# Expert tiles cut into three places of two turns, short VectorE operands moved to PSUM, and sorting spread over odd turns

## Chip, core and metric

The kernel runs on one core of a Trainium2 chip. The metric is the device time of one execution in microseconds; of several runs the median is given. Five engines work from queues of their own, each in order: TensorE (PE; its weight loads are the rows PEld), VectorE (DVE), ScalarE (ACT), GpSimd (POOL) and SyncE (SP), which here only issues DMAs.

## What is computed

Eight images of 256 channels and 32 x 32 places go through two layers. All is float32.

```python
# layer 0: deformable attention, 4 heads, 64 sampled keys per image
x = x + conv_attn(groupnorm(x))
#   logits get a bias per (query, key): a perceptron of width 64 on the
#   signed log distance, 2 -> 64 -> 64 -> 1, for 1024 x 64 pairs and 4 groups
# layer 1: on 1024 tokens of 256 per image
t = t + attn(layernorm(t))          # sigmoid(q t^T) t, no softmax
t = t + moe(layernorm(t))           # 8 experts 256 -> 256 -> 256, top 2 of a router
#   moe(u) = u + sum_e weight_e * (gelu(u w1[e] + b1[e]) w2[e] + b2[e])
```

The bias perceptron is most of the arithmetic.

## The kernel before

**Turns.** The main loop runs over 8 batches (images) of 64 turns. A turn does two steps of the bias perceptron. For each, a first layer `h1` of 128 x 1024 values is made two turns ahead: one by GpSimd (L471) with a ReLU on ScalarE (L476), one by VectorE (L469). TensorE runs the second layer, eight small products into the two PSUM buffers `h2p` (L484). They are emptied by ScalarE (L490) for the first kind and VectorE (L492) for the second. In even turns the third layer follows (`sim`, L511). A turn with nothing else on TensorE (an odd one, "bare" below) has 2 us of matmuls; an even one has 3.9. The perceptron's inputs `ta` and `nb` come by DMA every eight turns and are scaled in `scale` (L440 to L442) when the turn's number leaves 3 by 8: `ta` on ScalarE, `nb` on VectorE.

**Work beside it.** Everything else is cut into steps by generators (each `yield` ends a step), and the loop says which step stands at which turn. Every engine then works in exactly the order in which the program was written (`in_order`, L76); only the order of the scattering DMAs among themselves is free. In batch b these run:
- `prep` of batch b+1 (L236): group norm, queries, a 36-tap convolution on VectorE (L285, L287), offsets and sampling. `Side.step` (L1011) runs it and the softmaxes of batch b, from turn 5; while `sorting` is set, it runs no step of `prep`.
- `attention` of batch b-1 (L600): `to_query` (layer norm, transposes, projections), `slots` (the products `ap` and `vp`), `finish` (second layer norm, router logits), then `route` (L798), the sorting: it picks two experts per token, counts, and gives each token a slot. It is some 45 short VectorE operations on 8 to 168 columns, in six steps. Then 16 scattering DMAs on GpSimd (L781), one a turn, send the tokens to their slots.
- `experts` of batch b-2 (L893): 12 rounds of two tiles of 128 slots (the last batch: 15 of one tile of 256). Round n, as one step, runs `yp` for n-2 (L928; second product, emptied by VectorE's `yt`, L933), fetches and weight loads (L907, L914), `hp` for n-1 (L946; first product, emptied by the gelu `ht`, L954), and `tp` for n (L964; transposes, emptied by ScalarE's `xg`, L966).
- `combine` of the batch before that (L971): gathers on GpSimd (L999), VectorE's weighted sums (L991), transposes `op` (L982), stores. One step a turn.

`mix` (L1074) says when a step of `experts` is due: in batches 2 to 6 at turns 24, 26, 27, 29, 31 and 33 and at odd turns from 41 to 57, and the last at turn 9 of the next batch. It leaves out 35, 37 and 39, where the sorting stands. In batch 7 it runs a step at turns over 9 that are odd or divisible by 3. After turn 63 the tail does the last attention, sorting and experts.

All small matmul outputs (`psum`, L129) share a pool of two PSUM banks, taken in turn: each waits until what was written two takes before has been read. One more bank, `still` (L138), holds copies of `nb` in its first half; its second half (`shared`) is the convolution's and the sorting's workspace.

Of the kernel before, what the change touches and what calls it, by code (L numbers as in the profile page):

```python
# [9 lines left out]
F32 = mybir.dt.float32  # L10
I32 = mybir.dt.int32
AF = mybir.ActivationFunctionType
ALU = mybir.AluOpType
# [90 lines left out]
def tile_conv_attn_hybrid(ctx: ExitStack, tc: tile.TileContext, x, par, qw, w1, w2_, cst, out):  # L104
# [34 lines left out]
    held_nb = still[:, 0:256].rearrange("p (s g y) -> p s g y", g=2, y=16)  # L139
    shared = still[:, 256:512]  # L140
    attending = sorting = convolving = False

    def xin(b):
# [43 lines left out]


    ncb2 = cpool.tile([P, 1], F32, name="ncb2")
    nc.vector.tensor_scalar(ncb2, par_("cb2"), -1.0, None, ALU.mult)  # L190
# [45 lines left out]
    def prep(b, xb, st):  # L236
        qp = frames[b % 2]
        stats = small.tile([P, 2, 2, 6], F32, name="stats")
        mv = small.tile([P, 2, 2], F32, name="mv")
        for k in range(2):  # L240
            for h in range(2):
                nc.vector.bn_stats(stats[:, k, h, :], xb[:, k, halves(h)])
            nc.vector.bn_aggr(mv[:, k, :], stats[:, k, :, :].rearrange("p h s -> p (h s)"))
            yield
        gm = psum("gm")
        nc.tensor.matmul(gm[:, 0:2], lhsT=cst_("gavg"), rhs=mv[:, :, 0], start=True, stop=True)
        gmean = small.tile([P, 2], F32, name="gmean")
        nc.vector.tensor_copy(gmean, gm[:, 0:2])
        dm = small.tile([P, 2], F32, name="dm")
        nc.vector.tensor_sub(dm, mv[:, :, 0], gmean)  # L250
        nc.vector.tensor_mul(dm, dm, dm)
        nc.vector.tensor_add(dm, dm, mv[:, :, 1])
        yield
        gv = psum("gv")
        nc.tensor.matmul(gv[:, 0:2], lhsT=cst_("gavg"), rhs=dm, start=True, stop=True)
        grs = small.tile([P, 2], F32, name="grs")
# [169 lines left out]
    def terms(b, k, h, part):  # L426
        number = 4 * k + 2 * h + part
        fd = sts[b]["fd"].rearrange("k (s r) f -> k r s f", r=2)
        ta = abpool.tile([P, 16, 2, 32], F32, name="ta")
        nb = abpool.tile([P, 16, 2, 16], F32, name="nb")  # L430
        nc_ = abpool.tile([P, 2, 8, 16], F32, name="nc")
        taf = ta.rearrange("p s g x -> p s (g x)")
        nbf = nb.rearrange("p s g y -> p s (g y)")
        ss = slice(part * 16, (part + 1) * 16)
        for r in range(2):
            rs = slice(64 * r, 64 * r + 64)
            nc.sync.dma_start(out=taf[rs], in_=fd[k, r, ss, 0:64].partition_broadcast(64))
            nc.sync.dma_start(out=nbf[rs], in_=fd[k, r, ss, 64 + 32 * h : 96 + 32 * h].partition_broadcast(64))

        def scale():  # L440
            nc.scalar.activation(taf, taf, AF.Identity, bias=par_("cb1"), scale=par_("w1x"))
            nc.vector.tensor_scalar(nbf, nbf, par_("w1y"), -1.0, ALU.mult, ALU.mult)  # L442

        def second():
            cps = [psum("cp") for _ in range(2)]
            for r, g in ((0, 0), (1, 1), (0, 1), (1, 0)):
                rs, gs = slice(64 * r, 64 * r + 64), slice(64 * g, 64 * g + 64)
                nc.tensor.matmul(
                    cps[r][gs, 0:128], lhsT=par_("w2")[rs, gs], rhs=nb[rs, 1::2, g, :],
                    start=True, stop=True, tile_position=(64 * r, 64 * g),  # L450
                )
            for r in range(2):
                nc.scalar.activation(  # L453
                    nc_[:, r].rearrange("p s y -> p (s y)"), cps[r][:, 0:128], AF.Identity, bias=ncb2,
                )

        def hold(half):
            nc.scalar.copy(held_nb[:, 4 * half : 4 * half + 4], nb[:, 8 * half + 1 : 8 * half + 8 : 2])  # L458

        return (ta, nb, nc_, b, number), scale, second, hold  # L460
# [139 lines left out]
    def attention(b, st, o, rt):  # L600
# [8 lines left out]
        def to_query(h):  # L609
# [18 lines left out]
            yield  # L628
            mv = small.tile([P, 4, 2], F32, name="lmv")
            for u in range(4):  # L630
# [36 lines left out]
        def finish(q):  # L667
            mv = small.tile([P, 2, 2], F32, name="lmv2")
            for u in range(2):
# [83 lines left out]
        def rest():  # L753
# [20 lines left out]
            attending = sorting = True  # L774
            yield from route(lqs, rt, LARGE if b == NB - 1 else SMALL)
            attending = sorting = False

            xs, group = xss[b % 2], f"slots{b}"
            for n in range(16):
                m, c = divmod(n, 2)  # L780
                sent = nc.gpsimd.indirect_dma_start(  # L781
                    out=xs[:, :], out_offset=bass.IndirectOffsetOnAxis(ap=rt["slot"][:, c, m : m + 1], axis=0),
                    in_=ut[:, m, :], in_offset=None,
                )
                if n:
                    tc.declare_no_dep(sent.ins, group=group, reason="other slots")
                tc.add_to_no_dep_group(group, sent.ins)
                sents.add(sent.ins.name)
                yield
            rt.update(xs=xs, xu=xu)  # L790
# [7 lines left out]
    def route(lqs, rt, slots_):  # L798
# [8 lines left out]

        def part(n, size=64):
            a = shared[:, 64 * n : 64 * n + size]
            return a.rearrange("p (m e) -> p m e", e=E) if size == 64 else a  # L810

# [9 lines left out]
        def pick(name):  # L821
            m = one.tile([P, 8], F32, name="m" + name)
            nc.vector.tensor_reduce(m, lg, AX.X, ALU.max)
            eq, first = part(1), part(2, 8)
            nc.vector.tensor_tensor(eq, lg, wide(m), ALU.is_equal)
# [31 lines left out]
        )  # L857
        many = one.tile([P, E], F32, name="many")
        nc.vector.tensor_reduce(many, need, AX.X, ALU.add)
# [3 lines left out]
        nc.vector.tensor_reduce(ends[:, 1:9], part(1), AX.X, ALU.add)  # L863
        at = part(3)
        nc.vector.scalar_tensor_tensor(
# [3 lines left out]
        for c in range(2):  # L869
            nc.vector.tensor_scalar(ws[c], m1, 0.5 - c, 0.5, ALU.mult, ALU.add)  # L870
        place = one.tile([P, 2, 8], F32, name="place")
        for c, oh in enumerate((oh1, oh2)):
            nc.vector.tensor_tensor(part(1), at, oh, ALU.mult)
            nc.vector.tensor_reduce(place[:, c], part(1), AX.X, ALU.add)
        slot = held("slot", (P, 2, 8), I32)
        nc.vector.tensor_copy(slot, place)
        yield
# [4 lines left out]
        )  # L882
        whose = one.tile([P, TILES], F32, name="whose")
        nc.vector.tensor_reduce(whose, which, AX.X, ALU.add)
        expert = held("expert", (P, TILES), I32)
        nc.vector.tensor_copy(expert, whose)
        yield
        rt.update(slot=slot, expert=expert, w=ws)

# [3 lines left out]
    def experts(b, rt):  # L893
# [23 lines left out]
        fetch(0)  # L917
        yield
        fetch(1)
        first[0] = weights(0, w1pool, 2 * C + 2, w1, "w1")  # L920
        yield
        for n in range(rounds + 2):
            if n >= 2:
# [9 lines left out]
                nc.vector.tensor_tensor(yt, yp, f2[:, 0:several, 2 * C :].to_broadcast([P, 2, C]), ALU.add)  # L933
                nc.sync.dma_start(out=yv[at(n - 2), :].rearrange("(s p) c -> p s c", p=P), in_=yt)  # L934
            if n + 2 < rounds:
                fetch(n + 2)
# [20 lines left out]
            if n + 1 < rounds:  # L957
                first[n + 1] = weights(n + 1, w1pool, 2 * C + 2, w1, "w1")
            if n < rounds:
                xl = rows.pop(n)  # L960
# [5 lines left out]
                nc.scalar.copy(xg, tp)  # L966
            if n < rounds + 1:
                yield
        sums.append((b, combine(b, rt, yv)))
# [35 lines left out]
    class Side:  # L1005
# [5 lines left out]
        def step(self, both=True):  # L1011
            busy = False
            if self.waiting and not (sorting and self.busy):
                busy = self.busy
                self.busy = next(self.waiting[0], None)
                if self.busy is None:
                    self.waiting.pop(0)
                    self.busy = True
            if self.left and both and not busy and not sorting:
                self.left = next(self.prep, self) is not self  # L1020
# [52 lines left out]

    def mix(b, i):  # L1074
        of = mixtures[0][0] if mixtures else NB
        if of == b - 2 and b < NB - 1:
            due = i in (24, 26) or i > 26 and i % 2 and i not in (35, 37, 39, 59, 61, 63)
        elif of == b - 3:
            due = i == 9
        else:  # L1080
            due = b == NB - 1 and (i >= TURNS - 2 if of == b - 1 else of < b and i > 9 and (i % 2 or i % 3 == 0))
        if due:
            step(mixtures)

    def step(what):
        if what and next(what[0][1], what) is what:
            what.pop(0)

    for n in range(NB * TURNS):
        b, i = divmod(n, TURNS)  # L1090
        if i == 0:
            steps = iter(())
# [16 lines left out]
        if n % 8 == 6 and coming_ < total:  # L1109
            table = coming  # L1110
        new = []
        if n + 2 < NB * TURNS:
# [6 lines left out]
        if coming_ < total:  # L1119
# [5 lines left out]
            elif n % 8 == 6:  # L1125
                hold(1)
        if i > 4:
            side.step(i > (8 if b else 4))
# [7 lines left out]
        advance(mains)  # L1136
        mix(b, i)
        step(sums)
# [5 lines left out]
    while mains:  # L1144
        advance(mains)
        if sorted_ or not attending and n % 2:
            step(mixtures)
        sorted_ = sorted_ or sorting
        n += 1
    while mixtures:  # L1150
        step(mixtures)
        step(sums)
# [110 lines left out]
```

## Time and profile before

| what | value |
|---|---|
| median of 3 runs | 3119.95 us (3118.14 to 3121.78) |
| the profiled execution, its own time | 3118.0 us |
| its span, first to last instruction | 3116.2 us |
| head, up to the first second-layer matmul | 72.4 us |
| batches 0 to 7 (7: up to 6 us after turn 63 began) | 256.1, 320.6, 358.8, 366.1, 365.6, 369.3, 365.0, 372.8 us |
| tail | 269.6 us |
| granted TensorE clock, mean | 0.976 |
| GpSimd's L471, 128 x 1024, 512 times | 1916 ns each |
| VectorE's L469 and L492, 512 times each | 1212 and 1222 ns each |
| ScalarE's L476 and L490, 512 times each | 1051 and 1115 ns each |
| VectorE's L442 (`nb`), 64 times | 69.7 us, mean 1088, shortest 469, longest 2953 ns |

A page of the profile names a group of instructions by its line, engine, operation and tiles, as `out<-in`. It gives the time that the group was busy, the mean of one in ns, the idle time of its engine just ahead of it, and who ended that. A line of waits reads: who waited, for whom, us in total, how often, the longest. A line of the timeline reads: start and length in us, engine, line, operation, tiles, shape, how many in a row, and in brackets the idle time ahead of it with its releaser. A window's columns are busy times by engine with the number of instructions, then the clock, the share of DMA time and GB/s. Busy matmuls are modelled ends; idle time of an engine that is not the bound costs nothing.

### The profile page before, as it was taken

What the parts mean: (1) busy time and instruction counts of PE and PEld (TensorE: products, weight loads), DVE (VectorE), ACT (ScalarE), POOL (GpSimd) and SP (SyncE); (2) the same over time, 40 slices, a digit from 0 to 9 for tenths busy, and PEclk for the clock granted to TensorE, in tenths of its full rate; (3) what the DMA queues carried; (4) which work ended last, traced back from release to release, by engine and by line L of the source; (5) the groups of instructions that cost most, each with busy time, mean ns of one, the idle gap of its engine ahead of it and who ended that gap; (6) DMA issues with size and microseconds to landing.
All of it is one profiled execution on the core that took longest, in us unless ns stands there. A gap on an engine that the chain in (4) does not pass through costs nothing. (4 is left out here: it accounts for less than half of the span.)

```text
span 3116.2 us, 51813 instructions
## 1 busy us (share of the span) xinstructions
PE 2827.7 (91%) x19592; PEld 1397.0 (45%) x19592; DVE 1987.2 (64%) x3015; ACT 1851.2 (59%) x2662; POOL 1381.8 (44%) x945
## 2 busy tenths in 40 slices
PE   3889998899999999999999999999989999988965
PEld 2223443344445453544545444454545546425754
DVE  4887668765774777566775667757775564593212
ACT  3676655765676656765566665666567566555322
POOL 2554434643454544535454353545445343371132
PEclk7999999999999999999999999999999999999988
DMA  3321111211463234622346125542246245442376
GB/s 98 92 46 35 21 28 31 73 21 35 112 180 97 45 86 110 199 52 56 99 137 188 33 53 139 146 130 41 67 120 191 58 107 168 138 99 85 111 247 220
DMA packets 428297, 311.21 MB, mean 100 GB/s; under 512 B 284432, under 2 KB 368656, under 8 KB 428048
## 3 DMA queue, kind: packets, MB, share of 16 engines
q1 hardware_dynamic: 415472, 273.14, 32.9%
q0 software_dynamic: 12288, 33.57, 3.7%
q8 instruction: 154, 2.52, 0.4%
q10 hardware_dynamic: 288, 1.20, 0.1%
q14 instruction: 95, 0.78, 0.1%
HBM read 239.93 MB, written 67.90 MB: 99 GB/s over the span
## 5 line engine op out<-in xcount | busy, mean ns | idle before, releaser
L471 POOL TENSOR_TENSOR h<-ta,nb 128x1024 f32<-128x1024 f32 x512 | 980.5, 1916 | 1138.2 <-PE h2p L484 1040.4
L484 PE MATMUL h2p<-h,pr__101 64*64 64x512 f32 x8192 | 1023.1, 610 | 89.6 <-DVE h L492 60.7
L492 DVE TENSOR_TENSOR h<-h2p,nc 128x1024 f32<-128x1024 f32 x512 | 625.5, 1222 | 439.6 <-PE h2p L484 434.1
L490 ACT ACTIVATE h<-h2p,pr__101 128x1024 f32<-128x1024 f32 x512 | 571.0, 1115 | 474.9 <-PE h2p L484 473.7
L469 DVE TENSOR_TENSOR h<-ta,still 128x1024 f32<-128x1024 f32 x512 | 620.4, 1212 | 47.3 <-ACT still L458 44.4
L476 ACT ACTIVATE h<-h 128x1024 f32<-128x1024 f32 x512 | 538.0, 1051 | 34.5 <-POOL h L471 34.1
L484 PEld LDWEIGHTS h2p<-h,pr__101 64*64 64x64 f32 x8192 | 254.8, 133 | 619.5 <-issue 290.6
L511 PE MATMUL sim<-h,pr__101 128*32 128x512 f32 x4096 | 498.6, 605 | 0.0
L511 PEld LDWEIGHTS sim<-h,pr__101 128*32 128x32 f32 x4096 | 107.7, 110 | 367.7 <-issue 367.7
L717 PE MATMUL ap<-qt,tn 128*128 128x256 f32 x1024 | 251.1, 389 | 2.6 <-DVE x L739 1.0
L954 ACT ACTIVATE ht<-hp,w 128x128 f32<-128x128 f32 (+1 forms) x366 | 108.6, 377 | 242.0 <-PE hp L946 208.6
L727 PE MATMUL vp<-tt,sg 128*128 128x256 f32 x1024 | 233.0, 381 | 3.5 <-ACT nc L453 3.3
L928 PE MATMUL yp<-w,ht 128*128 128x256 f32 x792 | 198.4, 394 | 29.2 <-ACT ht L954 6.8
L717 PEld LDWEIGHTS ap<-qt,tn 128*128 128x128 f32 x1024 | 184.6, 190 | 86.9 <-issue 41.7
L999 POOL DMA_INDIRECT gs<-ys,slot x128 | 129.0, 1008 | 208.3 <-issue 64.9
L727 PEld LDWEIGHTS vp<-tt,sg 128*128 128x128 f32 x1024 | 193.2, 190 | 36.9 <-issue 5.7
L946 PE MATMUL hp<-xg,w 128*128 128x128 f32 (+1 forms) x1464 | 198.0, 288 | 12.0 <-PE yp L928 6.0
L739 DVE TENSOR_TENSOR x<-x,vp 128x512 f32<-128x512 f32 x64 | 44.0, 688 | 246.4 <-PE vp L727 246.4
L946 PEld LDWEIGHTS hp<-xg,w 128*128 128x128 f32 x1464 | 187.3, 194 | 29.3 <-PE yp L928 10.3
L928 PEld LDWEIGHTS yp<-w,ht 128*128 128x128 f32 x792 | 145.7, 193 | 87.5 <-issue 35.2
L933 DVE TENSOR_TENSOR yt<-yp,w 128x512 f32<-128x512 f32 x99 | 68.0, 687 | 167.6 <-PE yp L928 141.6
L735 ACT ACTIVATE sg<-ap 128x512 f32<-128x512 f32 x128 | 76.4, 598 | 148.0 <-PE ap L717 136.0
(270 smaller groups left out, 2611.1 us busy)
## 6 DMA issues: line engine op xcount, KB each, us to landing
w<-in_w SPq DMA_DIRECT2D x183, 384.0 KB
w<-in_w SPq DMA_DIRECT2D x183, 257.0 KB
ta<-fd SPq DMA_DIRECT2D x128, 256.0 KB
xl<-xs SPq DMA_DIRECT2D x99, 256.0 KB
ys<-yt SPq DMA_DIRECT2D x99, 256.0 KB
nb<-fd SPq DMA_DIRECT2D x128, 128.0 KB
xb<-in_x SPq DMA_DIRECT2D x8, 1024.0 KB
x<-in_x SPq DMA_DIRECT2D x8, 1024.0 KB
```

The source lines that it names most:

```text
L469: nc.vector.tensor_tensor(h1, a, b, ALU.max)
L471: nc.gpsimd.tensor_tensor(h1, a, b, ALU.subtract)
L476: nc.scalar.activation(h1, h1, AF.Relu)
L484: nc.tensor.matmul(h2p[gs, r, :], lhsT=par_("w2")[rs, gs], rhs=h1[rs, g].rearrange("p y x -> p (y x)"), start=True, stop=True, tile_positi ...
L490: nc.scalar.activation(h2, h2p, AF.Relu, bias=par_("cb2"))
L492: nc.vector.tensor_tensor(h2.rearrange("p r (y x) -> p r y x", x=W), h2p.rearrange("p r (y x) -> p r y x", x=W), nc_.unsqueeze(3).to_broad ...
L511: nc.tensor.matmul(sim[32 * q : 32 * q + 32, :], lhsT=par_("z3")[:, 15 - m : 47 - m], rhs=h2s[2 * u + q // 2][:, q % 2, :], start=False, s ...
L717: nc.tensor.matmul(ap[:, u, :], lhsT=tn[:, k, m0 : m0 + P], rhs=qt[:, k, quarter(q)], start=(k == 0), stop=(k == 1),)
L727: nc.tensor.matmul(vp[:, i, :], lhsT=sgs[s][:, u, i * P : (i + 1) * P], rhs=tt[:, 2 * todo[n - 2 + s][1] + u, :], start=(s == u == i == 0) ...
L928: nc.tensor.matmul(yp[:, s, :], lhsT=ht[:, f, s * P : (s + 1) * P], rhs=f2[:, s * several // 2, f * C : (f + 1) * C], start=(f == 0), stop ...
L946: nc.tensor.matmul(hp[:, f, us], lhsT=f1[:, u, k * C + f * P : k * C + (f + 1) * P], rhs=xg[:, k, us], start=(k == 0), stop=(k == 1),)
L999: nc.gpsimd.indirect_dma_start(out=got[m][:, c, :], out_offset=None, in_=yv[:, :], in_offset=bass.IndirectOffsetOnAxis(ap=slot[:, c, m : m ...
```

## The change

1. *Places of a tile.* `experts` yields three times a round: after `yp`, after `hp`, after `tp`. `mix` is called twice a turn, ahead of the turn's first and second layer (part 0) and at its end (part 1). In batches 2 to 6 the first fetches stand at turn 26. At each odd turn from 31 to 55, `yp` stands ahead of the second layer, fetches, weights and `hp` at the turn's end, and `tp` at the end of the next even turn. The last `yp` stands ahead of turn 9's second layer in the next batch. In batch 7 and in the tail, `whole()` runs three steps in one.
2. *Sorting.* `route` has five steps, at odd turns only (35 to 43), except in the tail. Its last part (which expert a tile has) runs between the second and third send. The sends start at turn 44. `Side.step` isn't run in the odd turns of the sorting, and `prep` is no longer held in the even ones.
3. *Short operands.* Twelve-column pieces `tiny` of `still`, and pieces `few` and `whose`, take the place of SBUF tiles: group means, layer norm statistics, the sorting's small vectors. The scaling of `nb` goes to ScalarE.

```diff
+    tiny = [still[:, 464 + 12 * n : 476 + 12 * n] for n in range(4)]
...
+        gmean, dm = tiny[3][:, 0:2], tiny[3][:, 2:4]
...
-        nc.vector.tensor_sub(dm, mv[:, :, 0], gmean)
-        nc.vector.tensor_mul(dm, dm, dm)
-        nc.vector.tensor_add(dm, dm, mv[:, :, 1])
+        nc.vector.tensor_sub(dm, mv[:, :, 0], gm[:, 0:2])
+        away = small.tile([P, 2], F32, name="away")
+        nc.vector.tensor_sub(away, mv[:, :, 0], gm[:, 0:2])
+        nc.vector.tensor_mul(dm, dm, away)
+        nc.vector.tensor_add(mv[:, :, 1], dm, mv[:, :, 1])
...
-            nc.vector.tensor_scalar(nbf, nbf, par_("w1y"), -1.0, ALU.mult, ALU.mult)
+            nc.scalar.activation(nbf, nbf, AF.Identity, scale=nw1y)
...
-            mv = small.tile([P, 4, 2], F32, name="lmv")
+            mv = tiny[2][:, 0:8].rearrange("p (u s) -> p u s", s=2)
...
-            yield from route(lqs, rt, LARGE if b == NB - 1 else SMALL)
+            steps = route(lqs, rt, LARGE if b == NB - 1 else SMALL)
+            for _ in range(5):
+                while b < NB - 1 and turn % 2 == 0:
+                    yield
+                next(steps)
+                yield
...
+                if n == 1:
+                    run(steps)
...
-            eq, first = part(1), part(2, 8)
+            eq, first = part(1), few(0)
...
-        many = one.tile([P, E], F32, name="many")
+        many = few(8)
...
-        place = one.tile([P, 2, 8], F32, name="place")
+        place = tiny[2][:, 0:8], tiny[3][:, 0:8]
...
-        whose = one.tile([P, TILES], F32, name="whose")
+        whose = shared[:, 168 : 168 + TILES]
...
         fetch(0)
-        yield
         fetch(1)
...
+            if n == rounds + 1:
+                break
+            yield
             if n + 2 < rounds:
                 fetch(n + 2)
...
                 first[n + 1] = weights(n + 1, w1pool, 2 * C + 2, w1, "w1")
+            yield
             if n < rounds:
...
-            if self.left and both and not busy and not sorting:
+            if self.left and both and not busy:
...
+    def mix(b, i, part):
         of = mixtures[0][0] if mixtures else NB
+        if b == NB - 1 and of >= b - 2:
+            if part and (i >= TURNS - 2 if of == b - 1 else i > 9 and (i % 2 or i % 3 == 0)):
+                whole()
+        elif of == b - 2:
+            if not part:
+                due = i in ODD
+            else:
+                due = i == 26 or i in ODD or i - 1 in ODD
+            if due:
+                step(mixtures)
+        elif of == b - 3 and i == 9 and not part:
+            step(mixtures)
+
+    ODD = (31, 33, 35, 37, 39, 41, 43, 45, 47, 49, 51, 53, 55)
...
+        mix(b, i, 0)
         new = []
...
-        if i > 4:
+        if i > 4 and not (sorting and i % 2):
             side.step(i > (8 if b else 4))
...
-        mix(b, i)
+        mix(b, i, 1)
```

## What was predicted

> **What bounds the kernel now.** I read the page's busy times first, then the windows of one batch, then TensorE's waits, then two timelines.
>
> ```profile
> PE 2827.7 (91%) x19592; PEld 1397.0 (45%) x19592; DVE 1987.2 (64%) x3015; ACT 1851.2 (59%) x2662; POOL 1381.8 (44%) x945
> PEclk7999999999999999999999999999999999999988
> ```
>
> TensorE has work for 2827.7 of 3116.2 us and runs at full clock; no other engine is over 64%. Where other work covers a turn, its 16 second-layer matmuls always take 1.95 us. So the kernel is bound by TensorE, and a change that leaves its matmuls alone can win at most its idle time: 3116.2 - 2827.7 = 288.5 us. By batch (windows from each batch's first second-layer matmul, length less PE busy) that is 47.0 in the head, 25.1, 24.4, 16.4, 18.3, 18.2, 20.3, 18.9 and 31.1 in batches 0 to 7, and 68.8 in the tail. Batch 4 by stretch (turns 8-12, 13-26, 27-33, 34-41, 42-58, 59-63):
>
> ```profile
> 1411.07:1440.19 29.12, 26.31 (x172) 10.36 (x172) 24.41 (x32) 18.51 (x24) 16.89 (x14) 0.94 0.15 46
> 1440.19:1527.42 87.23, 86.32 (x553) 45.01 (x552) 62.50 (x101) 49.31 (x65) 45.33 (x34) 1.00 0.32 77
> 1527.42:1569.94 42.52, 39.49 (x298) 21.71 (x297) 31.47 (x50) 25.61 (x41) 17.04 (x11) 1.00 0.49 135
> 1569.94:1608.29 38.35, 33.08 (x247) 11.93 (x247) 31.43 (x57) 24.53 (x36) 18.44 (x11) 0.96 0.34 87
> 1608.29:1711.45 103.16, 98.58 (x753) 54.78 (x752) 59.62 (x89) 70.58 (x119) 51.92 (x36) 1.00 0.64 183
> 1711.45:1739.60 28.15, 27.43 (x181) 13.26 (x177) 11.85 (x11) 18.67 (x27) 9.57 (x5) 1.00 0.22 51
> ```
>
> The columns are length, then busy PE, PEld, DVE, ACT, POOL, then clock. Idle is 2.8, 0.9, 3.0, 5.3, 4.6 and 0.7 us. The fourth stretch is the sorting: no tiles, VectorE busy for 31.4 of 38.35 us, the clock at 0.96. Who ends TensorE's waits:
>
> ```profile
> PE h2p L484 <- DVE h L492: 60.7, 53, 3.0
> PE h2p L484 <- ACT h L490: 27.1, 53, 3.7
> ...
> PE gm L246 <- ACT tn L647: 9.4, 4, 2.4
> ```
>
> The first two are turns in which TensorE has only the 2 us of second layer. It is back at its two `h2p` buffers before VectorE (L492) or ScalarE (L490) has emptied them. Turn 36 to 37 of batch 4, in the sorting:
>
> ```profile
> 1580.61 1.91 POOL L471 TENSOR_TENSOR h<-ta,nb 128x1024 f32<-128x1024 f32 x1 [0.47 <-PE h2p L484]
> 1580.80 2.00 DVE L442 TENSOR_SCALAR nb<-nb,pr__101 128x512 f32<-128x512 f32 x1
> ...
> 1584.51 1.21 DVE L469 TENSOR_TENSOR h<-ta,still 128x1024 f32<-128x1024 f32 x1
> ...
> 1585.64 1.22 DVE L492 TENSOR_TENSOR h<-h2p,nc 128x1024 f32<-128x1024 f32 x1
> ...
> 1586.92 1.09 PE L484 MATMUL h2p<-h,pr__101 64*64 64x512 f32 x8 [1.80 <-DVE h L492]
> ```
>
> L442 takes 2.00 us and ends just after the GpSimd operation that began before it; its shortest is 0.469. With eight short sorting operations behind it, L492 is late and TensorE waits 1.80 us.
>
> **The change part by part** (against the profiled execution: 3118.0 us, span 3116.2; the median of the runs shown, 3119.95, is 0.06% above it).
>
> *Places of a tile, batches 2 to 6.* A tile round costs TensorE 2.0 (yp, 198.4/99) + 2.0 (hp, 198.0/99) + 0.63 (tp, 62.2/99) us, all at the end of an odd turn now. After: yp ahead of the odd turn's second layer, hp behind it, tp in the even turn. Nothing is added on TensorE; the order says which waits lose their cause.
> - Sorting, turns 34-41. Odd turns become 2.0 + 1.95 + 2.0, about 6 us. VectorE then has yt 0.69 + L469 1.21 + L492 1.22 + a sorting part of about 2.1 = 5.2 us, and in the even turn (TensorE 3.95 + 0.63) about 4.2. It is early everywhere. I leave 1.0 us idle per batch (0.46 for `lp`'s bank, which now hits `tp`, and a new 0.47 behind `cp`). Idle now is 5.6, 5.3, 5.3, 7.6, 5.3; gain 24 us. The clock at 0.96 over 33 us of matmuls costs 1.3 more; I take 1.0 back per batch: 29 in all.
> - Turns 8-12. In batches 3 to 6 the last yp stands behind turn 9's second layer. Its rows then go to DRAM, the first gather queues on GpSimd for them (idle 6.6 us), L471 stands behind the gather, ScalarE's in-order queue behind L471, and `gm` waits 2.3 us; then the clock falls to 0.94 and the four `q1` products take 5.23 instead of 3.74 us. Batch 2, without that yp, takes 23.66 us here; 29.33, 29.12, 30.67, 27.70 in the others. With yp 2 us earlier, and yt ahead of 2.4 us of L469 and L492 on VectorE, the gather starts some 3 us earlier. Expected 23.66 + 1.9 = 25.6: gain 3.7 + 3.5 + 5.1 + 2.1 = 14.4.
> - Turns 42-58. Waits now: tp on yt 1.7, yp on xt 1.24, hp on yp 0.3 to 0.8. After: 0.47 (44), about 0.8 (47: `ov`, `tp`, then hp needs `ov`'s bank), 0.7 (52), 0.44 (58, since turn 57 is now bare) = 2.4 against 4.6: gain 11 over five batches.
> - Turns 27-33. Tiles start four turns later, so turns 27, 29 and 31 are bare. Batch 1, bare today, shows what that costs: 0.99 at turn 31 and 1.81 at 32, about 3.0 us with the rest. Now it is 3.0 too (2.4 in batch 2): -0.6.
>
> Sum 54.
>
> *Short operands.* L442 leaves VectorE: 69.7 us there (64 x 1088 ns). On ScalarE I price it by L607, the same shape: 0.706 us, so 64 x 0.71 = 45 us on an engine at 59%, in odd turns that an even one of at least 3.95 us on TensorE follows. The program also has 110 table loads for 101, 9 x 1.283 = 12 us, under the same cover; uncovered, both would be some 57 us, which is why ScalarE is a rival below. The other stalls: L251 median 1330 for 160 ns, L886 1340 for 178, L860 613 for 234; about 3 us a sorting and 1.2 a preparation. Operations that keep two SBUF operands (L836, L844 to L846, L879) keep theirs. Against this stands a rule of the Trainium skill, Perfetto Trace Analysis, Optimizing Scalar/DVE Operations: VectorE's access overhead is about 60 ns in SBUF and about 125 in PSUM. Some 45 operations a batch get a PSUM operand; by the rule that is 45 x 65 ns x 8 = 23 us more. The row nearest: 64 columns of two SBUF operands (L836) take 224 ns at best, with one in PSUM (L873) median 230. I take the row (2 us); by the rule the sum of VectorE would still fall by about 75 us. What reaches TensorE where no tile hides it: batch 1, where turns 34-45 need about 46 us of VectorE after (24 x 1.21, sorting 9, softmax 5, preparation 3) against 41 of TensorE, so 6 idle for 11 now: 5. Batch 0, VectorE-late in turns 16-29 with one or two L442: 3.
>
> *Batch 7 and tail.* Three steps are run in one there, so TensorE's cyclic order yp, hp, tp stays; only the phase moves, and two empty steps fall away. In batch 7 `op` behind hp no longer waits for hp's bank (0.8 to 2.1 us, four times) and turn 11 goes as above; turns 31 and 33 become bare (-3): 5. In the tail, two rounds (8.5 us) move ahead of `lp`, and sorting and sends start later by about that. But now the first product of the last tiles comes late for another reason:
>
> ```profile
> 2996.00 7.63 SPq L934 DMA_DIRECT2D ys<-yt  x2
> ...
> 3003.94 0.91 SPq L907 DMA_DIRECT2D xl<-xs  x2
> ...
> 3006.93 1.11 PE L964 MATMUL tp<-cs,xl 128*128 128x128 f32 x4 [4.43 <-DMA xl<-xs]
> ```
>
> SP fetches only after the last rows of the tiles before; the sends' last issue had ended at 2987.6. Fewer rounds are left behind `cnt`, so I expect the fetch at about 2987.6 + 7.5 + 2 = 2997: gain 5 (bounds -4, if the sends land as late behind their issue as the fetch does now, and +9). Head: the scaling behind `ta` on ScalarE, -0.7.
>
> **Sum.** 54 + 5 + 3 + 5 + 5 - 0.7 = 71. The new rotation of two PSUM banks over 60 rounds will make waits that no row shows. I charge the row hp on yp (0.36 and 0.81 in turns 45 and 49 of batch 4, so 1.2 a batch of 12 rounds) at 0.1 a round as the low end, yp on xt (1.24) as the high end, and take 0.27, near the low one: -16. Forecast: 3118 - 55 = 3063 profiled, 3065 as median.
>
> **Rivals.**
> - *More.* No new waits and the tail's upper bound: -75, 3045 or less; chance 0.09.
> - *Half is given back.* The bare turns 9, 31, 57 leave VectorE late, as in batch 1 (1.85 at turn 58 on top of 0.44), and batches 1 and 7 sort in bare odd turns with 4.5 us of VectorE in each. For it: batch 1's rows. Against: `kp` moves a turn earlier, so its 1.7 us of copies do not fall into turn 56. Also counted here: the stalls do not go away with one operand in PSUM, which costs 8. Some 30 less: 3085 to 3118, middle 3095; 0.23, of it 0.06 within 0.2%.
> - *Head of line, slower.* yp stands in TensorE's in-order queue ahead of the second layer, and yt on VectorE ahead of L469 and L492. If yp's bank (hp's, emptied by 1.5 us of gelu after a 1.28 table load on a fuller ScalarE) or its weights come late, everything behind waits in full. From 71/60 = 1.2 us a round it decides; at the dearest row, 1.24, plus ScalarE 0.15 late a round, it costs 83: about 3132. Against: between hp and the yp that takes its bank lies an even turn of 4.6 us, and weights are asked for two rounds (21 us) ahead. 0.12.
>
> **Numbers.** Likeliest case 3040 to 3085, 0.56, at 3065. A measurement can tell this kernel from no change only beyond about 0.2%, 6 us (3113.7 to 3126.2). Faster 0.56 + 0.09 + 0.17 = 0.82, same 0.06, slower 0.12. The range 3040 to 3108 leaves out the slow case and the ends of the others.
>
> **What would show it.** Right: batches 3 to 6 last about 356 us each (366 now) and all PE idle is near 235; turns 34-41 show about 1 us idle and clock 1.00; the wait of `gm` for `tn` is gone; `h2p` on `h` of DVE is under 35; VectorE's sum is near 1890; `nb` on ACT takes about 0.7; the last tiles' first `tp` comes within 165 us of the last turn's start (166.3 now). Wrong: new waits of yp or hp on ACT or DMA over 0.5 us a round, PE idle over 260, or ScalarE's `L490` as the main releaser of `h2p`.

## The result and the profile after

The changed kernel takes 3095.55 us (median of 5 runs, 3092.59 to 3104.16) beside 3119.95 of before on the same chip: a ratio of 0.9926, interval 0.9914 to 0.9937. That is faster by 24.4 us, inside the range, where 55 was forecast. The profiled execution took 3095.55 us, its span is 3093.7: 22.5 less than before.

The page of the changed kernel, busy times and the clock by slices:

```profile
PE 2816.0 (91%) x19592; PEld 1393.8 (45%) x19592; DVE 1897.3 (61%) x2968; ACT 1899.3 (61%) x2735; POOL 1382.0 (45%) x945
...
PEclk7999999999999999999999999999999999999988
```

VectorE lost 90 us (1890 was forecast), ScalarE won 48. TensorE's busy time fell by 11.7 with the same 19592 matmuls, at a mean clock of 0.979 for 0.976; its idle time fell from 288.5 to 277.7 only, where 235 was forecast. Batch 4 by the same stretches:

```profile
1408.29:1433.82 25.53, 24.62 (x173) 9.48 (x173) 19.39 (x32) 18.90 (x25) 16.94 (x14) 1.00 0.17 52
1433.82:1521.05 87.23, 86.38 (x554) 45.02 (x553) 61.22 (x100) 49.80 (x66) 45.33 (x34) 1.00 0.27 70
1521.05:1555.51 34.46, 30.65 (x237) 13.61 (x237) 29.44 (x47) 22.20 (x30) 16.65 (x11) 1.00 0.44 123
1555.51:1600.65 45.14, 43.15 (x332) 22.86 (x331) 26.98 (x49) 33.98 (x53) 15.31 (x8) 1.00 0.52 148
1600.65:1701.59 100.94, 96.47 (x728) 51.20 (x728) 60.24 (x98) 68.55 (x114) 52.88 (x38) 1.00 0.58 169
1701.59:1730.18 28.59, 27.42 (x180) 13.26 (x176) 11.46 (x10) 19.11 (x27) 11.71 (x7) 1.00 0.26 71
```

Tiles moved from the third stretch into the fourth, so only length less PE is comparable: idle is now 0.9, 0.8, 3.8, 2.0, 4.5 and 1.2 us. Turns 8-12 take the 25.5 us that were forecast at clock 1.00; the sorting's idle is 2.0 for 5.3, also at 1.00. But 42-58 has 4.5 as before (2.4 forecast), and the last stretch has grown. By part of the program, length and TensorE's idle time:

| part | before, us | after, us | idle before | idle after |
|---|---|---|---|---|
| head | 72.4 | 72.8 | 47.0 | 47.8 |
| batch 0 | 256.1 | 256.4 | 25.1 | 25.0 |
| batch 1 | 320.6 | 323.6 | 24.4 | 27.3 |
| batch 2 | 358.8 | 358.3 | 16.4 | 15.5 |
| batches 3 to 6, each | 365 to 369.3 | 359.6 | 18.2 to 20.3 | 14.7 |
| batch 7 | 372.8 | 376.7 | 31.1 | 35.7 |
| tail | 269.6 | 267.7 | 68.8 | 67.9 |

Batches 2 to 6 win 28.1, the tail 1.9; batches 1 and 7 lose 3.0 and 3.9. TensorE's own waits name what is new (who waited, for whom, us, times, longest):

```profile
PE h2p L490 <- DVE h L498: 55.5, 42, 4.5
...
PE h2p L490 <- ACT h L496: 25.5, 59, 1.3
...
PE tp L985 <- ACT nc L459: 8.6, 7, 1.5
PE q L660 <- ACT nc L459: 8.2, 7, 1.2
PE ov L574 <- ACT nc L459: 7.8, 7, 1.1
```

The first two are down by 5.2 and 1.6 us only. The rows of `nc` are of another kind. `nc` is ScalarE's copy (L459) of the product `cp` in turns 4, 12, 20 and so on; whoever takes `cp`'s PSUM bank next waits for it. All such waits sum to 48.4 us where before had 24.9. Turns 35 to 36 of batch 4, ScalarE and TensorE, show why:

```profile
1567.65 1.23 ACT L447 ACTIVATE ta<-ta,pr__101 128x1024 f32<-128x1024 f32 x1
...
1568.79 0.71 ACT L448 ACTIVATE nb<-nb,nw1y 128x512 f32<-128x512 f32 x1
...
1569.51 1.28 ACT L974 ACT_TABLE_LOAD   x1
...
1570.81 1.15 ACT L974 ACTIVATE ht<-hp,w 128x128 f32<-128x128 f32 x4
...
1571.82 1.13 ACT L496 ACTIVATE h<-h2p,pr__101 128x1024 f32<-128x1024 f32 x1
1572.24 0.45 PE L454 MATMUL cp<-nb,pr__101 64*64 64x128 f32 x8
...
1572.82 1.08 ACT L482 ACTIVATE h<-h 128x1024 f32<-128x1024 f32 x1
1573.77 0.65 ACT L459 ACTIVATE nc<-cp,ncb 128x128 f32<-128x128 f32 x2
1574.21 0.66 PE L985 MATMUL tp<-cs,xl 128*128 128x128 f32 x4 [1.52 <-ACT nc L459]
```

From 1567.65 on ScalarE has no gap. `nb` takes 0.71 us, as priced, but it stands in an unbroken queue ahead of the gelu (`ht`, with its table load), `L496`, `L482` and `nc`: `cp` is there at 1572.7, `nc` starts at 1573.77, and TensorE stands for 1.52 us. My forecast had 0.47 here.

### The profile page after: what moved, and what is told of

Its sections match the earlier page's. It is cut to its first block, busy times and chain, and to the rows that moved or that the text cites. A ratio compares the mean times of both kernels' runs of the same rounds, so it can differ in the third digit from the quotient of the medians.

```text
span 3093.7 us, 51788 instructions
## 1 busy us (share of the span) xinstructions
PE 2816.0 (91%) x19592; PEld 1393.8 (45%) x19592; DVE 1897.3 (61%) x2968; ACT 1899.3 (61%) x2735; POOL 1382.0 (45%) x945
## 5 line engine op out<-in xcount | busy, mean ns | idle before, releaser
L490 PE MATMUL h2p<-h,pr__101 64*64 64x512 f32 x8192 | 1011.9, 605 | 82.0 <-DVE h L498 55.5
L496 ACT ACTIVATE h<-h2p,pr__101 128x1024 f32<-128x1024 f32 x512 | 570.9, 1115 | 485.8 <-PE h2p L490 485.4
L482 ACT ACTIVATE h<-h 128x1024 f32<-128x1024 f32 x512 | 537.8, 1051 | 13.5 <-POOL h L477 13.2
L945 PE MATMUL yp<-w,ht 128*128 128x256 f32 x792 | 201.2, 398 | 25.5 <-ACT ht L974 7.0
L733 PEld LDWEIGHTS vp<-tt,sg 128*128 128x128 f32 x1024 | 193.5, 190 | 36.9 <-issue 5.7
L966 PEld LDWEIGHTS hp<-xg,w 128*128 128x128 f32 x1464 | 183.4, 193 | 45.7 <-issue 23.5
L745 DVE TENSOR_TENSOR x<-x,vp 128x512 f32<-128x512 f32 x64 | 44.0, 688 | 256.3 <-PE vp L733 256.3
```

Source lines behind the costliest of these rows:

```text
L482: nc.scalar.activation(h1, h1, AF.Relu)
L490: nc.tensor.matmul(h2p[gs, r, :], lhsT=par_("w2")[rs, gs], rhs=h1[rs, g].rearrange("p y x -> p (y x)"), start=True, stop=True, tile_positi ...
L496: nc.scalar.activation(h2, h2p, AF.Relu, bias=par_("cb2"))
L733: nc.tensor.matmul(vp[:, i, :], lhsT=sgs[s][:, u, i * P : (i + 1) * P], rhs=tt[:, 2 * todo[n - 2 + s][1] + u, :], start=(s == u == i == 0) ...
L945: nc.tensor.matmul(yp[:, s, :], lhsT=ht[:, f, s * P : (s + 1) * P], rhs=f2[:, s * several // 2, f * C : (f + 1) * C], start=(f == 0), stop ...
L966: nc.tensor.matmul(hp[:, f, us], lhsT=f1[:, u, k * C + f * P : k * C + (f + 1) * P], rhs=xg[:, k, us], start=(k == 0), stop=(k == 1),)
```

## Experiments

Kernels sent together ran on one chip, and only those are compared in time: before itself takes about 3120 us on some chips and 3104 on others (last experiment), while the changed kernel takes 3094 to 3097 on both. Where an experiment stands on another chip than the changed kernel, I go by idle times from the profiles. Those of the changed kernel agree, between four profiles, within 0.3 us in each of batches 2 to 6 and 2.1 us in batch 7; those of before, between three, within 2.6 and 3.7.

**nb back on VectorE** (`e1_nb_dve`).

```diff
-            nc.scalar.activation(nbf, nbf, AF.Identity, scale=nw1y)
+            nc.vector.tensor_scalar(nbf, nbf, par_("w1y"), -1.0, ALU.mult, ALU.mult)
```

> The changed kernel with the scaling of nb back on VectorE; all else stays. Theory A: on ScalarE the scaling stands between ta's and the gelu of the tiles, so that the copies nc of the next turn come late (1.1 us of TensorE wait in turn 4, 1.5 in 36, 1.6 in 52, 1.2 in 60 of batches 2 to 6, where before had at most 0.7). Then these waits fall to 0.5, batches 3 to 6 win about 3 us each, but VectorE gets its 1 to 3 us stalls beside GpSimd back, in batches 0, 1, 7 above all: 3085 to 3095. Theory B: what is missing is due to the tiles' three places on two PSUM banks, and nc is only named because it ends last; then nothing is won and the stalls come on top: 3100 to 3110.

3090.67 beside 3103.59 of before (0.9960, 0.9946 to 0.9973). The time is in theory A's range. Waits on `nc` fall to 36.9 us, all idle time to 272.8. Batches 3, 4 and 6 do not win the 3 us of theory A (14.5 to 14.6 us idle for 14.7), because a stall comes back in turn 11, where VectorE's `nb` runs beside GpSimd. In batch 4:

```profile
1421.73 2.72 DVE L448 TENSOR_SCALAR nb<-nb,pr__101 128x512 f32<-128x512 f32 x1
1422.24 1.92 POOL L477 TENSOR_TENSOR h<-ta,nb 128x1024 f32<-128x1024 f32 x1
...
1424.84 3.28 PE L660 MATMUL q<-tn,qwt 128*128 128x512 f32 x4 [2.30 <-DVE away L256]
```

So ScalarE's version gives away somewhat more than it saves. But 36.9 is still 12 above before, with `nb` back where it was: that half comes with the new places of the tiles. By the lines of turn 35 above it is the gelu, which now stands at that turn's end too; no run moves the gelu alone.

**ta's scaling behind nc** (`e2_ta_later`): `ta` is scaled when n % 8 is 5, `nb` stays at 3.

> The changed kernel, nb still scaled on ScalarE in turn 3 of 8, but ta's scaling (1.23 us) moved from turn 3 to turn 5, behind the copies nc: the same work, in another order. Theory A (nc late behind ta, nb and a gelu): the waits for nc in turns 4, 36, 52 and 60 go to 0.5 or less, 2 to 3 us a batch, together 16 to 20: 3075 to 3080. Theory B (the two PSUM banks): within 4 us of the changed kernel's 3095.6.

3086.07 beside 3103.59 (0.9942, 0.9929 to 0.9956). The wait at turn 36 is 0.47, at 4 and 60 too, at 52 it is 0.51, and batches 3 to 6 have 12.2 us idle each (14.7). That is A's mechanism: the same work on ScalarE, in another order. A's total, 3075 to 3080, was missed: batch 0 loses 3.6 us of idle time (28.6 for 25.0), by a wait in turn 32. Three lines from there, of `e9_three` (below), which has the same wait:

```profile
187.56 7.87 POOL L479 TENSOR_TENSOR h<-ta,nb 128x1024 f32<-128x1024 f32 x4 [7.96 <-ACT ta L450]
...
189.79 3.88 DVE L320 SCALAR_TENSOR_TENSOR gk<-gk,cs 128x256 f32<-128x256 f32 x2
...
198.75 1.98 PE L492 MATMUL h2p<-h,pr__101 64*64 64x512 f32 x8 [5.62 <-DVE h L500]
```

Held up by `ta`, GpSimd runs four operations on end, and VectorE's two L320 beside it take 3.88 us; in the changed kernel, with GpSimd idle, they take 0.75.

**Order yp, hp, tp** (`e3_phase`).

```diff
         first[0] = weights(0, w1pool, 2 * C + 2, w1, "w1")
-        yield
+        if b < NB - 3:
+            yield
```

> The changed kernel with one place less at the start of the tiles in batch 7 and in the tail, so that three steps run as yp, hp, tp there, as before the change, and not as tp, yp, hp. Theory C: the order tp, yp, hp makes xg late for hp and puts yp and tp behind the banks of ap and vp; then batch 7 wins about 5 us and the tail 1 to 3: 3087 to 3091. Rival D: batch 7 is slower because its sorting stands in bare odd turns with VectorE held beside GpSimd (turns 35 to 58); then the order does nothing: 3094 to 3097.

3081.54 beside 3103.59 (0.9931, 0.9917 to 0.9944), under C's 3087 to 3091. Batch 7 has 31.2 us idle for 35.7, and lasts 371.2 for 376.7; the tail lasts 261.1 for 267.7. So C holds against D, and the order costs more than C said. What it does in the changed kernel, turn 17:

```profile
2546.74 0.60 PE L985 MATMUL tp<-cs,xl 128*128 128x128 f32 x4
...
2548.25 0.59 ACT L987 COPY xg<-tp 128x512 f32<-128x512 f32 x1
...
2548.89 1.99 PE L945 MATMUL yp<-w,ht 128*128 128x256 f32 x8 [1.55 <-ACT xg L987]
```

Four such waits for `xg` (turns 12, 17, 21 and 25: 0.73, 1.55, 1.28 and 0.43 us) are gone.

**nb on ScalarE, in the kernel before** (`e5_before_nb_act`): the one line of `scale`.

> The kernel before with one edit: nb is scaled on ScalarE. The prediction's own step: some 70 us leave VectorE, ScalarE's 57 are covered; batches 0, 1, 7 and the sorting win 8 to 15 us: 3105 to 3112. Theory A: the copies nc in turns 28, 44 and 52 come 0.7 us late behind it, which takes 8 to 10 us back: 3112 to 3122.

3114.70 beside 3103.59 (1.0037, 1.0024 to 1.0049): 11 us slower. VectorE's sum falls by 65 us, waits on `nc` rise from 24.9 to 34.1, and what VectorE gains does not reach TensorE where it should: the sorting of batch 4 now waits 3.30 us in turn 40 where before waits 1.80 and 1.47 in turns 37 and 41. This step of mine, forecast as a gain, is a loss by itself.

**The changed kernel again, and edits together** (`e6_after_again`, `e7_both`, `e8_sort_every`, `e9_three`; before 3122.18).

> The changed kernel itself once more, beside the next three. If the gains of the two edits tried so far (ta's scaling behind nc, and the order yp, hp, tp) are real, it is slower than each of them: 3086 to 3096 where before has 3104 to 3120. If what they showed was only another chip's day, it stands at 3080 to 3085.

3096.36 (0.9917): it stands where it was.

> The changed kernel with two edits together: ta's scaling moved to turn 5 of 8, and the order yp, hp, tp in batch 7 and the tail. Theories A and C together: the gains add, since they lie in different batches: 12 to 22 below the changed kernel of the same runs. Rival: batch 7 has its own waits for sg, x and VectorE, which take up what the other edit gives: under 10 below it.

3076.57, 19.8 below the changed kernel: A and C add.

> The changed kernel with the sorting of batches 1 and 7 (where no tiles stand beside it) in consecutive turns and no prep within it, as before the change; batches 2 to 6 stay. Theory E: in batches 1 and 7 the bare odd turns hold 5 to 6 us of VectorE against 2 us of TensorE, and prep moved in between them (a 2.0 us operation beside GpSimd, then 4.5 us of wait at turn 38): batch 1 wins 3, batch 7 up to 2: 3 to 5 below the changed kernel. Theory F: VectorE is late by the sum of its work there, wherever it stands: within 2 of it.

```diff
-                while b < NB - 1 and turn % 2 == 0:
+                while 1 <= b < NB - 2 and turn % 2 == 0:
...
-        if i > 4 and not (sorting and i % 2):
+        if i > 4 and not (sorting and i % 2 and 1 < b < NB - 1):
...
-            if self.left and both and not busy:
+            if self.left and both and not busy and not (sorting and b == 1):
```

3096.69, the same: by the time, theory F's case. In the profile batch 1 wins (24.1 idle for 26.4 to 27.3), batch 7 does not (39.7 for 35.7 to 37.8). E can hold for batch 1 alone. What stands there in the changed kernel, turns 37 to 38:

```profile
521.99 1.95 POOL L477 TENSOR_TENSOR h<-ta,nb 128x1024 f32<-128x1024 f32 x1 [2.08 <-ACT still L464]
522.21 2.08 DVE L324 TENSOR_SCALAR gk<-gk 128x640 f32<-128x640 f32 x1
...
524.33 2.02 DVE L328 TENSOR_SCALAR ft<-gk,cs 128x128 f32<-128x128 f32 x1
...
528.66 1.98 PE L490 MATMUL h2p<-h,pr__101 64*64 64x512 f32 x8 [4.49 <-DVE h L498]
```

L324 and L328 are `prep`'s, let into the sorting by the change: 0.49 and 0.29 us in batch 4, 2.08 and 2.02 here, beside a GpSimd operation each.

> The three edits together (ta's scaling behind nc; yp, hp, tp in batch 7 and the tail; the sorting of batches 1 and 7 in consecutive turns). If they are independent: their sum, 15 to 25 below the changed kernel of the same runs, and batches 3 to 6 at 357 us each. If one takes another's place: no better than the best two.

3067.65 (0.9826, 0.9813 to 0.9840), 28.7 below the changed kernel: more than the sum, since batch 7 has 26.3 idle with all three.

**nb earlier; parts alone; tiles from turn 29** (before 3103.24).

> As the version with three edits, but nb's scaling is moved a turn earlier (turn 2 of 8) and ta's stays in turn 3. Theory A: what counts is that not both stand ahead of nc; nc's waits stay near 0.5, and batch 0 loses the 5.6 us wait of turn 32 that ta's late scaling gave it (GpSimd ran four operations on end behind ta, and VectorE's operations beside it took 4 to 6 times as long): 3060 to 3065 where that version had 3067.7. Rival: batch 0's wait has another cause, and ta alone ahead of nc already makes it late: 3067 to 3075.

3070.52. Batch 0 is back at 24.1 us idle, as said, but batches 3 to 6 have 12.9 to 13.1 for 12.2, and the total is the rival's: `ta` alone ahead of `nc` does cost something.

> Parts 1 and 2 of the change alone (places of the tiles, sorting at odd turns), with nb on VectorE and all short operands in SBUF tiles as before. The prediction's sum for these parts: 54 + 5 (batch 7) + 5 (tail) - 16 = 48 less than before. Theory A: about as fast as the whole change, since part 3 gives away in nc what it wins on VectorE: 22 to 30 less than before. Rival: part 3 carries the gain, and places alone give under 15.

3093.55 (0.9967, 0.9956 to 0.9979). By the number, 9.7, that is the rival's case; but on such a chip the whole change wins only 8 (last experiment), and the 22 to 30 had been named for the other. By the profile, idle time is 275.0 for the whole change's 277.7, and waits on `nc` are 36.6. So part 3 as made is worth nothing in sum, where 8 was forecast: places and sorting carry the result.

> Before, with the short operands in PSUM alone; nb stays on VectorE. The prediction: the short operations no longer stall beside GpSimd, 3 us a sorting and 1.2 a preparation, of which up to 8 us reach TensorE: 2 to 8 less than before. By the skill's rule of a dearer PSUM access: 45 operations a batch at 65 ns, of which at most the sorting's reach TensorE: 0 to 5 more. Rival: neither is on the path: within 2.

3098.98 (0.9984, 0.9977 to 0.9990): 4.3 less, as predicted. VectorE's sum is 1967.3 for 1987.2, with 16 operations more, and batch 1 has 20.8 us idle for 24.4. Two operations, before and here (times, then shortest, median and longest ns):

```profile
L581 DVE TENSOR_SCALAR lrs<-lmv x48: 169/170/1948, 295.1 to 2938.7; 128x2 f32<-128x2 f32 x32, 128x4 f32<-128x4 f32 x16
L583 DVE TENSOR_SCALAR lrs<-still x48: 159/160/163, 297.0 to 2929.8; 128x2 f32<-128x2 f32 x32, 128x4 f32<-128x4 f32 x16
...
L886 DVE CAST expert<-whose x8: 178/1340/2518, 538.5 to 2972.6; 128x24 int32<-128x24 f32 x8
L891 DVE CAST expert<-still x8: 182/182/183, 537.2 to 2964.1; 128x24 int32<-128x24 f32 x8
```

The long ones are gone, and the shortest is 10 ns less or 4 more with the operand in PSUM. So the dearer PSUM access of the Trainium skill (Perfetto Trace Analysis, Optimizing Scalar/DVE Operations), 65 ns by its figures, does not show.

> The version with three edits, the tiles two turns earlier: odd turns 29 to 53, the first fetches at turn 24. Theory H: a bare odd turn costs where VectorE has prep's long operations (turn 31 and 32: 1.07 and 1.81 us a batch); with tiles there from 29 on these waits go, batches 2 to 6 win 1.5 to 2.8 each: 7 to 14 less than the version with three edits. Rival: turn 55 is bare now and late instead, as 57 and 58 in batch 1 (2.2 and up to 1.7): within 3 of it, or slower.

3080.80 where its base had 3067.65 on another chip, and `e10_nb_earlier` 3070.52 on this one; by the profile, batches 3 to 6 have 13.1 to 13.5 us idle for 12.2. H's first half holds: turns 31 and 32 wait 0.50 and 0.24. But turns 57 and 58, now behind bare 55 and 57, wait 2.20 and 1.74. The cost moved, as the rival said.

**One cause alone, and the best version** (`e14_before_again` to `e17_batch0`; before 3121.79).

> The kernel before, for its profile on this chip. If chips differ in the granted clock or in the tail (where transfers decide), its batches 0 to 7 last as in the first profile and the tail differs by up to 9 us from 269.6; if the order of work differs, its idle time in batches 3 to 6 does.

One execution, 3128.0: batch 3 is 3.7 us longer than at first, the other batches within 1.6, the tail is 274.9. It also corrects a reading of the prediction. Turns 8-12 of batch 4:

```profile
1417.23:1444.83 27.60, 24.72 (x172) 9.65 (x172) 24.43 (x32) 18.39 (x24) 16.90 (x14) 1.00 0.17 48
```

`gm` waits 2.30 us here as it did in the first profile (2.29), but the clock stays at 1.00, and the stretch is 1.5 us shorter. In batch 3 of the same execution the wait is 2.33, the clock 0.89, the stretch 30.63. So the fall of the clock behind this wait comes in some executions and not in others.

> The changed kernel, beside the next. 3090 to 3097 on any chip if its batches are bound by its own waits; 3075 to 3082 if this chip is one on which before takes 3103 and the changed kernel gains as much there.

3094.22 (0.9910).

> The changed kernel with nb's scaling a turn earlier (turn 2 of 8) and nothing else changed. Theory A: nc's extra waits (3.3 us a batch in 2 to 6, 1 to 2 in the others) go: 10 to 18 less than the changed kernel beside it, batches 3 to 6 at 358. Theory B (the two PSUM banks): within 3 of it.

```diff
-            if n % 8 == 3:
-                scale()
+            if n % 8 == 2:
+                scale()
+            elif n % 8 == 3:
+                scale_ta()
```

3082.93, 11.3 less; batches 3 to 6 last 358.0 us. The same place in its profile:

```profile
1562.96 1.23 ACT L450 ACTIVATE ta<-ta,pr__101 128x1024 f32<-128x1024 f32 x1
...
1564.20 1.28 ACT L976 ACT_TABLE_LOAD   x1
1565.50 1.14 ACT L976 ACTIVATE ht<-hp,w 128x128 f32<-128x128 f32 x4
...
1568.45 0.65 ACT L461 ACTIVATE nc<-cp,ncb 128x128 f32<-128x128 f32 x2
1568.90 0.66 PE L987 MATMUL tp<-cs,xl 128*128 128x128 f32 x4 [0.90 <-ACT nc L461]
```

0.90 for 1.52, and only `nb` has left the queue. Waits on `nc` are 35.5 us for 48.4 (50.1 in `e15_after_third`): 13 to 15 us of idle time, 11.3 of time. B falls.

> The version with three edits, but batch 0 keeps ta's scaling in turn 3. If its 5.6 us wait in turn 32 came from ta's late scaling (GpSimd's operations bunched behind it and VectorE's beside them took longer): batch 0 back at 256 to 257 for 261, 3062 to 3065 in all where that version had 3067.7. Rival: batch 0 stays at 261.

3065.69 (0.9819, 0.9806 to 0.9833), just over the range. Batch 0 is at 256.3, so its wait did come from `ta`. But the gain over the changed kernel, 28.5, is that of `e9_three` (28.7), and all idle time is 251.2 for 251.3: what batch 0 wins (24.9 for 28.4), batch 1 loses (23.9 for 21.0), though no edit touches it.

**Where before differs by chip** (`e18_before_third`, `e19_after_fourth`).

> The kernel before. 3103 or 3120 by the chip; if 3103, the profile shows the missing 16 us in the tail (260 for 269.6 us) and in batches 3 to 6 (363 to 365 for 365 to 369).

3105.28. Its tail lasts 257.9 us for 269.6; the rest is spread over the batches, at most 4 us in one.

> The changed kernel. If before's order alone is sensitive to the chip: 3090 to 3097 also where before has 3103; if the chip gives both the same: 3075 to 3082 there.

3097.18, a ratio of 0.9974 (0.9966 to 0.9983): on this chip the change wins 8 us, not 24. The tail of the changed kernel is 267.0 on it, 267.7 on the first. Before, on the first chip and on this one, in the tail's sends:

```profile
2971.04 10.10 SPq L914 DMA_DIRECT2D w<-in_w  x4
...
2978.86 3.78 PE L928 MATMUL yp<-w,ht 128*128 128x256 f32 x8 [4.62 <-issue]
```

```profile
2967.30 4.15 SPq L914 DMA_DIRECT2D w<-in_w  x4
```

On the first chip four weight loads sit 10.1 us in SP's queue while GpSimd scatters, and TensorE then stalls by 4.62, 2.72 and 2.04 us; on this one they take 4.15, and up to the last tiles no stall of TensorE is longer than 2.12. Why the chips differ stays open.

## Why the forecast was right in sign and wrong in size

The forecast missed 33 us of profiled time: 10 in batches 2 to 6, 9 in batch 7, 8 in batch 1, 3 each in batch 0 and the tail. No single step covers all of it; the largest is the one on ScalarE. By its own steps:

- *Turns 8-12: right, in part by luck.* 25.5 us at clock 1.00, `gm`'s wait gone. But 1.5 to 3 us of the gain in each of batches 3, 4 and 5 was a clock that need not have fallen (`e14_before_again`), and the cause was only half of it: in `e1_nb_dve`, with `yp` moved and `nb` on VectorE, turn 11 of batches 3, 4 and 6 still stalls by 2.3 us, and in `e5_before_nb_act`, the other way round, `gm` still waits 2.3. Both had to go.
- *Sorting: right but for `nc`.* 2.0 us idle, of which 1.52 at turn 36 was priced at 0.47.
- *PSUM rotation, -16: too high.* New waits of `yp`, `hp` and `tp`, those on `nc` left out, are 2.3 us in batch 4 (0.47, 0.24 five times, 0.67). But the 0.47 (turn 44) and the 0.67 (turn 47) were already in the forecast for turns 42-58; left are 1.2 a batch, some 6 in all if the other batches are like it. The 10 charged too much hide part of the next step's miss.
- *Short operands on ScalarE: the step that failed.* I took `nb` as free "on an engine at 59%, in odd turns that an even one of at least 3.95 us on TensorE follows". The price of one `nb`, 0.71, was right. Not looked at was what is queued behind it: where a tile's gelu with its table load follows, ScalarE has no gap up to `nc`. Waits on `nc` grew by 23.5 us, 19.7 of it in batches 2 to 6, where the sum had room for 3.5 (0.47 in turn 36, 0.7 for 0.47 in turn 52). Of the 23.5, 12.9 leave when `nb` alone moves (`e16_nb_earlier`, 11.3 us of time). The rest comes with the tiles' new places, which bring a gelu into the same queue behind the old turn of `ta`: it stays with `nb` on VectorE (`e1_nb_dve`, 36.9), and goes for the most part with `ta` behind `nc` (`e2_ta_later`, 30.8). The uncovered price that I had set at 57 was too high, but zero was wrong.
- *Batch 7, +5: wrong, -3.9.* I wrote that "TensorE's cyclic order yp, hp, tp stays; only the phase moves". The phase is what counts: with the first fetches a place of their own, a `whole()` runs `tp`, `yp`, `hp`, so that `hp` needs the `xg` of the `tp` in the same step, not of the step before. The old order gives 5.5 back; with `nc` and the sorting mended too, batch 7 has 25.4 us idle (31.1 before), the gain that I had promised.
- *Batch 1, +5: wrong, -3.* Short operands alone give 3.7 (`e12_short_alone`). The whole change has 6.5 us more idle than that. The sorting in bare turns with `prep` between is 2 to 3 of it (`e8_sort_every`); this is the rival "Half is given back", for one batch of the two it named. Waits on `nc` are 1.4, and turns 57 and 58 wait 4.0 us for 1.9. Moving `ta` alone also helps (22.6, `e2_ta_later`), and `e17_batch0` and `e9_three`, alike in this batch, differ by 2.9; so the cause here is only in part shown.
- *Batch 0, +3: wrong.* It appears in no version. In turns 18 to 28 TensorE waits for VectorE as before (1.67, 1.80, 1.16, 1.16 us for 1.66, 1.83, 1.14, 1.16): `L442` was not what made it late.
- *Tail, +5: 1.9, and -9 on the other chip.* The step that failed is the delay of the sends: they begin 139.6 us after turn 63's start for 126.9, 12.7 later and not 8.5, and in the sum for the fetch only 7.5. Their 16 issues, one every 1.28 us, then set the fetch:

```profile
2978.84 0.97 POOL L793 DMA_INDIRECT xs<-ut,slot  x1 [0.31 <-issue]
...
2981.40 0.87 SPq L925 DMA_DIRECT2D xl<-xs  x2
...
2984.18 1.11 PE L985 MATMUL tp<-cs,xl 128*128 128x128 f32 x4 [13.49 <-DMA xl<-xs]
```

The landing itself was as priced: the fetch comes 1.6 us after the last issue has ended, for 2. The last tiles' first `tp`, at 164.1 us for 166.3, was within the 165 that I had named. On the other kind of chip before has no such stalls among the sends, its tail is 257.9, and the change loses 9 us there.

Of the rivals, head of line fell: no `yp` ahead of the second layer waits more than 0.24 us in batch 4. Half given back came closest, and its 3095 is the number measured, but by luck: the bare turns that it leaned on cost what the forecast already had in batches 2 to 6 (1.06 and 1.81 us in turns 31 and 32 of batch 4) and more than that in batch 1 alone; ScalarE's queue and batch 7's order made the rest.

## What to carry to other kernels

Work that moves to an engine with idle time is free only if nothing short stands behind it for which the bounding engine waits: follow that engine's queue from the moved instruction to the next operation that frees a buffer, in each turn in which it occurs. A moved 0.71 us, 64 times, cost 11 us of time here, and moving it one turn earlier won them back. And a step that runs in a loop has a first instruction: turning its phase changes which wait is next, even with the same cycle.

## Not expected of the hardware

That some VectorE operations are slow beside a GpSimd operation was priced for the short ones and `nb`. It also holds for `prep`'s (L324 0.49 and 2.08 us, L328 0.29 and 2.02: 4 to 7 times as long), and on which of them it falls changes with a shift of time: moving `ta` on ScalarE brought a wait of 5.62 us into a batch that it was not meant for. And one program, with one order of instructions, has two levels 16 us apart on different chips, the larger part of it in one stretch of scattering DMAs.
